# One graph-attention kernel: left and right projection as a 6x3x3-block product in 40 block products, in place of two 3x2x3 products in 15 each

## The chip, the cores and the metric

The kernel runs on one core of a Trainium2 chip. The metric is the device time of one execution in microseconds (us). Before the change it is 2752.59 us, the median of three runs (2751.57 to 2752.73).

## What is computed

128 graphs of 64 nodes with 768 features; two layers, then the input is added. All in float32. Of the reference only this matters here:

```python
h = max(layernorm(x), 0)
for l in range(2):
    m_left  = h @ W_left[l].T              # the two projections that are changed
    m_right = h @ W_right[l].T
    u_left  = h @ m_left^T / sqrt(768)     # 64 x 64 for each graph
    u_right = h @ m_right^T / sqrt(768)
    u = u_left on the upper triangle and the diagonal of adj, u_right below it
    attention = exp(u) * adj, rows scaled to sum 1
    h = relu(layernorm(attention @ (h @ W_lin[l].T + b_lin[l])) * ln_a[l] + ln_b[l])
out = x + h
```

## The kernel before

The engines are TensorE (PE; PEld is its weight loading), VectorE (DVE), ScalarE (ACT), GpSimd (POOL) and SyncE (SP, which issues the DMAs).

**Passes.** A layer has two passes over the 8192 tokens, in 16 blocks of 512. `pass_one` projects a block to the left and to the right, makes the scores (PE at L463, tile `aux`) and the softmax, and leaves the attention weights in DRAM. `pass_two` makes the linear projection (L852) and the product with the attention (`context`, L660, and `context_block`, L683), and normalizes. The second pass stays as it is, but for the places of its sums and loads.

**A projection as 15 block products.** Features are cut in three parts of 256, and a block of 512 tokens in two parts of 256, so a projection is a 3x3 matrix of weight blocks times a 3x2 matrix of token blocks: 18 block products. The kernel does it in 15, on sums and differences of blocks. `W_SUMS` makes 17 sums of weight blocks (L155, tiles `w_l`, `w_r`, `w_n`), `T_SUMS` 11 sums of token blocks (L155, tile `ts`, on POOL but in the first block), and `ORDER` lists the 15 products with the outputs that each one is added to or taken from. A product is four matmuls of 128x128 weights on 256 columns (L436). The right projection leaves out the last node of each graph, where the strict lower triangle has no use for it: 252 columns, in all blocks but the last. `read` (L203, L155) brings a PSUM sum into the tile `m`: the first contribution to an output is a copy on ACT, the others are additions on DVE (one operand in PSUM, one in SBUF).

**Order.** There is no automatic scheduler: instructions are issued as the Python code runs. `run(slot)` is called twice for each product and issues what `put` has entered for that slot, or the next entry of the list `idle`. So `prepare` sets the normalization of later blocks (`x`, statistics L238, transposes L380 into `xb`, the store `h<-xb` and the load `ht<-h`) beside the products. `one_aside` and `two_aside` put the loading and summing of later weights in `idle`, over many blocks. The scores of a block come after the first product of the next one. In layer 0 the first block's four token transposes on PE (L357) come ahead of its first product.

**End of a layer.** The scores of the last block follow its last product directly; then the linear products begin. The last context of layer 0 (L660) uses the PSUM places `aux`, which ACT and DVE read (L805, L823, L821) while the first products of layer 1 already run in `X`.

Of the kernel before, what the change touches and what calls it, by code (L numbers as in the profile page):

```python
# [17 lines left out]
def kernel(  # L18
# [12 lines left out]

# [37 lines left out]
    NBB = T // S  # L69
    adj_t = adj2.rearrange("(n h s) j k i -> n h j s (k i)", h=PAIR, s=Q)  # L70
# [9 lines left out]
    def put_all(slot, fs, step=1):  # L80
        for f in fs:
            if f is not None:
                put(slot, f)
            slot += step
        return slot

# [26 lines left out]
    FIRST = {0: ("X", 5), 1: ("Z", 8), 3: ("Y", 1), 5: ("V", 6), 9: ("V", 7), 12: ("V", 13)}  # L113
    W = {}
# [6 lines left out]
    def load_w(l, kind):  # L121
        v = SRC[kind][l].rearrange("(c p) o -> p c o", p=P)
        t = W[l, kind] = [wpool.tile([P, K2, D], F32, name=f"w_{kind}_{s}") for s in range(len(ORDER))]

        def load(s, i, j):
            nc.sync.dma_start(t[s], v[:, j * K2:(j + 1) * K2, i * D:(i + 1) * D])

        if (l, kind) in ((0, "l"), (0, "r")):
            return [lambda s=s, ij=ij: load(s, *ij) for s, ij in RAW.items()]
        return [lambda s=s, ij=ij: paced(t[s][:, 0, :1], lambda: load(s, *ij)) for s, ij in RAW.items()]  # L130

    def centre(l):

        t = W[l, "n"]
        for j in range(3):
            blocks = [s for s, (_, jj) in RAW.items() if jj == j]
            m = stat.tile([P, 3, K2], F32, name="wm", bufs=2)

            mean = stat.tile([P, K2], F32, name="wmm", bufs=2)
# [5 lines left out]
            idle.extend(none * (6 if j == 0 else 2))  # L145
            for n, s in enumerate(blocks):
                idle.append(lambda n=n, s=s, m=m: nc.vector.reduce_sum(m[:, n], t[s], axis=mybir.AxisListType.X))
            idle.append(mean_of)
            for s in blocks:
                idle.extend(none * 3)  # L150
                idle.append(lambda s=s, mean=mean: nc.gpsimd.tensor_sub(
                    t[s], t[s], mean.unsqueeze(2).to_broadcast([P, K2, D])))

# [3 lines left out]
    def sums_w(l, kind, eng):  # L157
        t = W[l, kind]
        return [lambda o=o, s=s, a=a, b=b: added(eng, t[o], s, t[a], t[b]) for o, s, a, b in W_SUMS]
# [9 lines left out]
    def tokens_of(key):  # L169
        ht = HT[key]  # L170
        r = {f"B{2 * j + t}": ht[:, j * K2:(j + 1) * K2, t * TH:(t + 1) * TH] for j in range(3) for t in range(2)}
        r.update(TS.get(key, {}))
        return r

    def sums_t(key, eng=nc.gpsimd):
        ts = TS[key] = {}

        def one(o, s, m, n):
            t = big.tile([P, K2, TH], F32, name="ts", bufs=13)
# [32 lines left out]
    KEPT = [[dram.tile([P, C, T], F32, name=f"h{l}_{u}") for u in range(NB)] for l in range(L)]  # L212
    ROWS = [dram.tile([NBB, S, H], F32, name=f"z_{u}") for u in range(NB)]
    ATT = [[dram.tile([P, Q, S], F32, name=f"att{l}_{u}") for u in range(NB)] for l in range(L)]
# [50 lines left out]

    def load_h(which, l, u):
        ht = HT[which, l, u] = big.tile([P, C, T], F32, name="ht")
        nc.sync.dma_start(ht, KEPT[l][u])

    def affine(which, l, u, step=1):  # L270

        def part(c0):
            for c in range(c0, c0 + step):
                ht = HT[which, l, u][:, c, :]
                nc.scalar.activation(ht, ht, AF.Relu, bias=cols[1][:, c:c + 1], scale=cols[0][:, c:c + 1])  # L275

        return [lambda c=c: part(c) for c in range(0, C if l else 0, step)]

    def transpose_rows(l, u, pool):

        key, xr, todo = (1, l, u), XR[l, u], []
        if l == 0:
# [24 lines left out]
            stats = [lambda q=q: mean_var(mv[:, q, :], [xr[q][:, :HH], xr[q][:, HH:]]) for q in range(Q)]  # L307
            norms = [lambda q=q: norm(q) for q in range(Q)]
            if u == 1:
# [3 lines left out]
                total, ss = (stat.tile([P, Q], F32, name=n, bufs=1) for n in ("total", "ss0"))  # L313
# [31 lines left out]
        if (l, u) == (0, 0):  # L345
            ht = HT[key] = big.tile([P, C, T], F32, name="ht")

            def turn(n, q):

                if n < 2:  # L350
                    p = ps_aux.tile([P, 2, T], F32, name="aux")
                    banks = [p[:, 0], p[:, 1]]
                else:
                    banks = [ps_st.tile([P, 2 * TH], F32, name=m) for m in ("XY", "ZV")[n - 2]]
                for m, p in enumerate(banks):
# [3 lines left out]
                for m, p in enumerate(banks):  # L359
                    to = ht[:, 3 * m:3 * m + 3].rearrange("p c (a g s) -> p g c a s", a=4, g=2)  # L360
                    to = to[:, q // 2, :, q % 2 * 2:q % 2 * 2 + 2, :]
                    (nc.vector.tensor_copy if n == 1 or n < m else nc.scalar.copy)(
                        to, p[:, :3 * P].rearrange("p (c a s) -> p c a s", c=3, a=2))

            for n, q in list(enumerate(START))[1:]:
                todo.append(lambda n=n, q=q: turn(n, q))
            todo.append(lambda: nc.sync.dma_start(KEPT[l][u], ht))
            return todo

        if (l, u) != (0, 1):  # L370
            xb = pool.tile([P, H // 32, Q, 32], F32, name="xb", bufs=1)

        def store():
            to = KEPT[l][u].rearrange("(b i) c t -> i c b t", b=4)
            for a in range(4):
                nc.sync.dma_start(to[:, :, :, a * P:(a + 1) * P],
                                  xb[a * 32:(a + 1) * 32].rearrange("i (c b) q j -> i c b (q j)", b=4))

        for q in range(Q):
            todo.append(lambda q=q: nc.vector.transpose(  # L380
                xb[:, :, q, :], xr[q].rearrange("p (b j) -> p b j", j=32)))
            todo.extend(none * ((l, u) != (0, 1)))
# [9 lines left out]
    def pass_one(l, aside):  # L392
        with tc.tile_pool(name=f"one{l}", bufs=2, reuse_waits="tile") as sp:
            ADJ, CHAIN, M = {}, {}, {}


            shapes = {"x": ([P, 2, H], 2), "xb": ([P, H // 32, Q, 32], 1), "m": ([P, C, NBB, 2, S], 1),
                      "adj": ([P, Q, 2, S], 2), "wm": ([P, Q, 2, S], 1)}
            places(sp, shapes, ("m", "adj", "x", "xb", "wm") if l else ("x", "xb", "m", "adj", "wm"))

            def load_adj(u):
                ADJ[u] = sp.tile([P, Q, 2, S], F32, name="adj")
                for h in range(PAIR):
                    nc.sync.dma_start(ADJ[u][h * S:(h + 1) * S].rearrange("p s k i -> p s (k i)"), adj_t[u, h])

            def softmax(u):
                return [lambda: next(CHAIN[u], None)] * 8

            def prepare(u):

                todo = transpose_rows(l, u, sp)
                todo.append(lambda: load_h(1, l, u))
                if u + 1 < NB:
                    todo.append(lambda: load_rows(l, u + 1, sp))
                todo.extend(softmax(u - 2) if u > 1 else [])
                todo.append(lambda: load_adj(u))
                todo.extend(none * ((9 if u > 1 else 15) if l else 0))
                return todo + affine(1, l, u)

            def project(u, k, just):  # L420


                b, w = lambda: tokens_of((1, l, u)), W[l, "lr"[k]]
                bank, seen = {}, set()


                ns = S - 1 if k and u < NB - 1 else S
                bs = "p (b s) -> p b s"
                for i, (at, t, _) in ((i, (o[1], o[2], o[3])) for i, o in enumerate(ORDER)):
                    new = i in FIRST  # L430
                    if new:
                        bank[at] = ps_st.tile([P, 2 * TH], F32, name=at)
                    p = bank[at][:, :NBB * ns].rearrange("p (g b s) -> p g b s", g=2, s=ns)
                    for g in range(2):
                        for c in range(K2):
                            nc.tensor.matmul(p[:, g], w[ORDER[i][0]][:, c, g * P:(g + 1) * P],  # L436
                                             b()[t][:, c, :].rearrange(bs, s=S)[:, :, :ns],
                                             start=(new and g == c == 0), stop=(c == K2 - 1), skip_group_check=True)
                        if g == 0:
                            run(30 * k + 2 * i)  # L440
                    if i == 0 and k == 0:
                        if u:
                            scores(u - 1)
                        M[u] = sp.tile([P, C, NBB, 2, S], F32, name="m", bufs=1)
                    read(p, lambda o: M[u][:, o // 2 * K2:(o // 2 + 1) * K2, o % 2 * 4:o % 2 * 4 + 4, k, :ns],
                         i, seen)
                    for f in just.get(i, ()):
                        f()
                    run(30 * k + 2 * i + 1)

            def scores(u):

                ht, m, adj = HT[1, l, u], M[u], ADJ[u]
                p = ps_aux.tile([P, 2, T], F32, name="aux")[:, 0].rearrange("p (q m) -> p q m", q=Q)
                for q in range(Q):
# [504 lines left out]
```

## Time and profile before

| | |
|---|---|
| median of 3 runs | 2752.59 us |
| profiled execution: span from first to last instruction | 2750.9 us |
| PE busy | 2730.4 us, 99% |
| DVE busy | 1345.6 us, 49% |
| POOL busy | 1194.4 us, 43% |
| ACT busy | 849.9 us, 31% |
| mean granted TensorE clock | 0.999 |

The profile gives for each engine the busy time and its groups of instructions (line, engine, operation, tile written <- tiles read, shapes, count; then the busy time, the mean of one in ns, and the idle time ahead of them with what ended it). The chain of waits goes from the last instruction back to whatever released each one. The timeline lists instructions in order of time: start, duration, engine, line, count, and in brackets the idle time before. An `x8` of PE in the chain is four matmuls with their four weight loads.

### The profile page before, as it was taken

The numbers are of one execution on the slowest core, as the hardware profiler recorded it, in microseconds if no ns is written. First come the engines' busy times: TensorE is split into PE (matmuls) and PEld (weight loads), VectorE is DVE, ScalarE is ACT, GpSimd is POOL, SyncE is SP. The second block draws the span as 40 slices with busy tenths as digits, with TensorE's granted clock in tenths as the row PEclk, the third lists the DMA queues.
The fourth block names the chain that finished last, engine by engine and source line by source line (L and its number), as shares of the span: only waits on it lengthen the run. The fifth ranks groups of instructions, "written<-read, shape, count | busy, mean of one in ns | idle before, by whom it ended". The sixth has DMA issues, their size and how long they took to land.

```text
span 2750.9 us, 46440 instructions
## 1 busy us (share of the span) xinstructions
PE 2730.4 (99%) x18746; PEld 2343.1 (85%) x18746; DVE 1345.6 (49%) x2266; ACT 849.9 (31%) x1612; POOL 1194.4 (43%) x937
## 2 busy tenths in 40 slices
PE   9999999999999999999999999999999999999998
PEld 8888888888888888888788888888888888888886
DVE  6555445545454333333435444444444335666667
ACT  3222223222221154444621211121122214544443
POOL 3332452223223555555522444223222325887886
PEclk9999999999999999999999999999999999999999
DMA  7434433343332333343555433443344205555555
GB/s 206 118 75 98 123 80 81 91 120 89 76 79 74 102 106 119 119 146 127 150 128 148 100 76 76 109 118 79 76 97 120 61 26 146 161 169 167 169 165 150
DMA packets 234072, 310.82 MB, mean 113 GB/s; under 512 B 54146, under 2 KB 184450, under 8 KB 225666
## 3 DMA queue, kind: packets, MB, share of 16 engines
q1 hardware_dynamic: 233698, 307.45, 41.8%
q8 instruction: 149, 2.44, 0.4%
q14 instruction: 65, 0.53, 0.1%
q10 hardware_dynamic: 160, 0.39, 0.0%
HBM read 202.91 MB, written 104.86 MB: 112 GB/s over the span
## 4 chain that ended last, share of the span: by engine, by line
PE 97%; DVE 1%; ACT 1%; DMA 0%; issue 0%; SPq 0%; DVEq 0%; ACTq 0%
PE X L436 24%; PE V L436 16%; PE X L852 12%; PE Y L436 12%; PE Z L436 8%; PE V L852 8%; PE Y L852 6%; PE aux L463 5%; PE Z L852 4%; PE aux L660 2%; PE aux L683 1%; PE Y L683 0%; ACT xb L316 0%; DVE wm L477 0%; DMA w_l<-in_w_left_dram 0%
## 5 line engine op out<-in xcount | busy, mean ns | idle before, releaser
L155 POOL TENSOR_TENSOR ts<-ht 128x512 f32<-128x512 f32 x441 | 587.0, 1341 | 1223.6 <-DMA ht<-h 565.1
L203 ACT ACTIVATE m<-X 128x512 f32<-128x512 f32 (+1 forms) x256 | 151.6, 592 | 1087.6 <-PE X L436 569.7
L155 POOL TENSOR_TENSOR ts<-ht,ts 128x512 f32<-128x512 f32 x189 | 248.7, 1323 | 135.6 <-PE X L852 60.5
L155 DVE TENSOR_TENSOR m<-m,V 128x512 f32<-128x512 f32 (+1 forms) x256 | 173.3, 677 | 269.1 <-PE V L436 269.0
L155 DVE TENSOR_TENSOR m<-m,X 128x512 f32<-128x512 f32 (+1 forms) x256 | 162.9, 677 | 248.0 <-PE X L436 247.4
L852 PE MATMUL X<-w_n,ts 128*128 128x256 f32 x1024 | 244.3, 380 | 0.8 <-ACT hl L203 0.6
L436 PE MATMUL X<-ts,w_l 128*128 128x256 f32 x1024 | 242.7, 380 | 0.1
L436 PE MATMUL X<-ts,w_r 128*128 128x252 f32 (+1 forms) x1024 | 238.8, 376 | 0.0
L155 DVE TENSOR_TENSOR m<-m,Z 128x512 f32<-128x512 f32 (+1 forms) x128 | 87.5, 683 | 307.7 <-ACT m L203 248.9
L852 PEld LDWEIGHTS X<-w_n,ts 128*128 128x128 f32 x1024 | 191.5, 190 | 33.3 <-issue 3.6
L436 PEld LDWEIGHTS X<-ts,w_l 128*128 128x128 f32 x1024 | 192.0, 190 | 30.1 <-DVE m L155 2.7
L436 PEld LDWEIGHTS X<-ts,w_r 128*128 128x128 f32 x1024 | 192.0, 190 | 26.0
L275 ACT ACTIVATE ht<-ht,b_col,a_col 128x512 f32<-128x512 f32 x192 | 143.5, 804 | 148.8 <-DMA ht<-h 148.8
L852 PE MATMUL Y<-w_n,ts 128*128 128x256 f32 x768 | 182.5, 379 | 0.0
L436 PE MATMUL Y<-ts,w_l 128*128 128x256 f32 x768 | 181.5, 379 | 0.6 <-DVE w_l L155 0.6
L436 PE MATMUL Y<-ts,w_r 128*128 128x252 f32 (+1 forms) x768 | 179.1, 376 | 0.0
L436 PEld LDWEIGHTS Y<-ts,w_l 128*128 128x128 f32 x768 | 145.8, 190 | 20.8 <-DVE w_l L155 1.0
L852 PEld LDWEIGHTS Y<-w_n,ts 128*128 128x128 f32 x768 | 145.8, 190 | 20.4 <-issue 0.6
L436 PEld LDWEIGHTS Y<-ts,w_r 128*128 128x128 f32 x768 | 145.9, 190 | 17.4
L155 DVE TENSOR_TENSOR hl<-hl,V 128x512 f32<-128x512 f32 (+1 forms) x136 | 89.1, 655 | 129.6 <-PE V L852 112.0
L818 POOL TENSOR_TENSOR z<-z,b 128x768 f32<-128x768 f32 x62 | 112.6, 1828 | 76.2 <-DVE z L815 76.2
L203 ACT ACTIVATE hl<-X 128x512 f32<-128x512 f32 (+1 forms) x135 | 77.9, 577 | 219.4 <-PE X L852 216.5
(167 smaller groups left out, 4737.1 us busy)
## 6 DMA issues: line engine op xcount, KB each, us to landing
ht<-h SPq DMA_DIRECT2D x63, 1536.0 KB, 7.1
h<-xb SPq DMA_DIRECT2D x124, 384.0 KB, 6.0
z<-z SPq DMA_DIRECT2D x128, 192.0 KB, 3.1
x<-z SPq DMA_DIRECT2D x128, 192.0 KB, 8.4
x<-in_x_dram SPq DMA_DIRECT2D x120, 192.0 KB, 8.3
xr<-in_x_dram SPq DMA_DIRECT2D x120, 192.0 KB, 3.8
out_dram<-xr SPq DMA_DIRECT2D x120, 192.0 KB, 2.7
adj<-in_adj_dram SPq DMA_DIRECT2D x64, 128.0 KB, 2.7
```

What stands on the lines that cost most here:

```text
L155: (eng.tensor_add if sign == "+" else eng.tensor_sub)(o, a, b)
L203: nc.scalar.activation(to(o), p, AF.Copy, scale=1.0 if sign == "+" else -1.0)
L275: nc.scalar.activation(ht, ht, AF.Relu, bias=cols[1][:, c:c + 1], scale=cols[0][:, c:c + 1])
L436: nc.tensor.matmul(p[:, g], w[ORDER[i][0]][:, c, g * P:(g + 1) * P], b()[t][:, c, :].rearrange(bs, s=S)[:, :, :ns], start=(new and g == c ...
L463: nc.tensor.matmul(p[h * S + e:h * S + e + 32, q, e:e + 95], ht[:, c, b * S + e:b * S + e + 32], mb[:, e:e + 95], start=(c == 0), stop=(c ...
L660: nc.tensor.matmul(cx[k][i, m, :HH], at[j, q, :], hl[j, q, m * HH:(m + 1) * HH], start=True, stop=True)
L683: nc.tensor.matmul(parts[r, k][n][i], at[j, q, :], hl[j, q, cut], start=True, stop=True)
L818: nc.gpsimd.tensor_add(zs[k], zs[k], rows["b"])
L852: nc.tensor.matmul(p[:, n], b[t][:, c, r * P:(r + 1) * P], w[s][:, c, :], start=(i in FIRST and i not in PRELOAD and n == c == 0), stop=(c ...
```

## The change

Left and right are now computed together: six rows of weight blocks (three left, three right) by three, times a 3x3 matrix of token blocks. That needs a superblock of 768 tokens and 54 block products, which `PRODUCTS` does in 40. The 16 blocks become 32 parts of 256 tokens: `SUPER[0]` is parts 0 and 1, done plainly in 36 products on the raw weights, and ten superblocks of three parts follow. The pieces:

- `W_OPS`: 101 sums of weight blocks, many with a factor, made once a layer from the 18 raw blocks. Class `Weights` gives them out while the plain block's products are issued, to DVE and POOL by two counted clocks (`turn_of`); those with a factor (51) go to DVE as `scalar_tensor_tensor`.
- `T_OPS`: 38 sums of token blocks for each superblock, all on POOL, at most 11 alive (class `Tokens`).
- `READS`: 84 contributions of products to the 18 outputs, 18 of them copies on ACT. The accumulators stay in PSUM over a superblock: product i goes on in bank i mod 4, with six banks in turn. So product i + 4 waits for the reads of product i.
- `m` becomes three tiles, `m0`, `m1`, `m2`. The scores of a superblock come after product 3 of the next one, and reads of products 0 to 3 after the scores.
- `REG`: 51 shared places of 128x512 for raw weights, weight sums, token sums and linear weights, handed on through the list `free`.
- The linear weights and the bias are loaded, centred and summed in the last superblock (`final`); centring moves from POOL to DVE and half of the 17 sums too.
- Left and right have all 256 columns. Token tiles, loads and stores go by parts; `aux` holds two of the six banks and the scores.

The diff, cut to its core (`...` marks what is left out; the tables are shortened to their first entries):

```diff
+    PRODUCTS = (
+        (74, 9), (71, 12), (82, 13), (78, 16), (72, 17), (67, 19), (73, 21), (89, 23), (75, 15), (76, 25), (60, 8),
...
+    READS = (
+        ((10, -2), (11, -1)), ((6, -2), (8, 1), (11, -1)), ((5, -1),), ((14, 1), (15, -1), (16, -2), (17, -2)),
...
+    T_OPS = (
+        (9, 4, 7, "-"), (10, 1, 7, "+"), (11, 2, 8, "+"), (12, 10, 11, "+"), (13, 3, 6, "-"), (14, 4, 5, "+"),
...
+    W_OPS = (
+        (18, 0, 1, 2, -1), (19, 8, -2, 5, 1), (20, 10, -2, 4, 1), (21, 6, -2, 3, 1), (22, 13, 1, 14, 1),
...
+    CHAINS, BANKS = 4, 6
+    SUPER = [(0, 1)] + [tuple(range(p, p + 3)) for p in range(2, NP, 3)]
+    PLAIN = 36
+    SCORED = 3
+    REGS = 51
+    REG = [wpool.tile([P, K2, D], F32, name=f"g{i}") for i in range(REGS)]
+    free = deque(REG)
...
+        def emit(self, eng, op):
+            v, a, ca, b, cb = op
+            x, y = self.at[a], self.at[b]
+            t, dead = self.place(v, a, b)
...
+            if ca == 1:
+                added(eng, t, "+" if cb > 0 else "-", x, y)
+            else:
+                nc.vector.scalar_tensor_tensor(t, x, float(ca), y, op0=ALU.mult,
+                                               op1=ALU.add if cb > 0 else ALU.subtract)
...
-            def project(u, k, just):
-                ns = S - 1 if k and u < NB - 1 else S
-                for i, (at, t, _) in ((i, (o[1], o[2], o[3])) for i, o in enumerate(ORDER)):
-                    new = i in FIRST
-                    if new:
-                        bank[at] = ps_st.tile([P, 2 * TH], F32, name=at)
...
-                    if i == 0 and k == 0:
-                        if u:
-                            scores(u - 1)
...
+            def turn_of(slot):
+                now = slot * 0.86
+                clock["vector"] = max(clock["vector"], now - 1.0) + sum(getattr(f, "vector", 0.0) for f in plan.get(slot, ()))
+                run(slot)
+                if weights.left and slot >= start["weights"]:
+                    while clock["vector"] <= now and weights.some(nc.vector):
+                        clock["vector"] += 0.62
+                    if clock["pool"] <= now and slot < start["tokens"]:
+                        if weights.some(nc.gpsimd, 40):
+                            clock["pool"] = max(clock["pool"], now) + 1.35
+                if clock["pool"] <= now + 1.5 and tokens.step(slot):
+                    clock["pool"] = max(clock["pool"], now) + 1.35
...
+            order = [(0, 0), (1, 0), (0, 1), (1, 1)] + [(w, t) for w in range(2, 6) for t in range(2)]
+            for n, (w, t) in enumerate(order):
+                if n == 2 and mid:
+                    mid()
+                bank = bank_of(n)
+                for j in range(3):
+                    tok = HT[1, l, t][:, j * K2:(j + 1) * K2, :]
+                    product(bank, weights.at[3 * w + j], tok, j == 0, slot)
...
+            for k in range(1, len(SUPER)):
+                put_all(slot + 2 * SCORED + 4, softmax(k - 1), 3)
+                if k == last:
+                    final(slot, tokens)
...
+                for i, (f, t) in enumerate(PRODUCTS):
+                    w, tok = weights.need(f), tokens.need(k, t)
+                    product(bank_of(CHAINS * (k - 1) + i % CHAINS), w, tok, i < CHAINS, slot)
+                    tokens.used(k, t)
...
+                    if i == SCORED:
+                        scores(k - 1)
...
+                    if i >= SCORED:
+                        for n in waiting:
+                            reads(n)
+                        waiting = []
+                    turn_of(slot + 1)
+                    slot += 2
...
+        def final(slot, tokens):
+            put_all(slot + 6, load_n(l), 2)
+            put(slot + 12, lambda: load_h(2, l, 0))
...
+            put_all(slot + 24, affine(2, l, 0), 2)
+            put_all(slot + 30, centre(l) + sums_n(l))
+            put_sums_t((2, l, 0), slot + 56, 2, slot + 50)
...
-    pass_one(0, {1: one_aside(0)})
-    pass_two(0, {1: two_aside("l"), 2: two_aside("r")})
-    pass_one(1, {1: one_aside(1)})
+    pass_one(0, {"weights": 7, "tokens": 58, 1: 13, 2: 38}, final_of(0))
+    pass_two(0, {11: lambda: later(load_raw(1), 1)})
+    pass_one(1, {"weights": 0, "tokens": 50, 1: 8, 2: 24}, final_of(1))
```

In the changed program the projection is at L619, the scores at L641, sums and additions at L231, weight sums with a factor at L523, reads with a factor 2 at L806, first reads at L802. A slot is half a product; a superblock has 80.

More of the change, by code (lines that the diff above doesn't have):

```diff
@@ L580, in pass_one, with bank_of @@
-            for f in list(idle):
-                if f:
+            KEEP["scores"] = KEEP["aux", 1]
+            def bank_of(n):
+                n %= BANKS
+                return KEEP["aux", 0][:, n] if n < 2 else KEEP["XYZV"[n - 2]]
+            flat = M[2].rearrange("p c b k s -> p (c b k s)")
+            spare = [flat[:, n * K2 * D:(n + 1) * K2 * D].rearrange("p (c d) -> p c d", c=K2) for n in range(6)]
+            weights, tokens = Weights(l, spare), Tokens(l)
+            clock = {"pool": 0.0, "vector": 0.0}
@@ L582, in pass_one @@
+            for n in sorted(plan):
+                for f in plan.pop(n):
                     f()
-            idle.clear()
             AHEAD.append(fresh(l, 0, (0, 1)))
-            scores(NB - 1)
-            for f in softmax(NB - 1):
+            scores(last)
+            for f in softmax(last):
                 f()
@@ L595, in bias @@
     def bias(l):
[L598 to L600 removed]
+        ab = [free.popleft() for _ in range(2)]
+        W[l, "bias"] = ab
+        t = rows["bias", l] = [ab[n // 2][:, n % 2, :] for n in range(4)]
+        todo = [lambda i=i, to=to: row(f"b{i}", b_lin[l], i * D, (i + 1) * D, t[to]) for i, to in enumerate((1, 2, 0))]
         bm = stat.tile([P, 3], F32, name="bm", bufs=1)
```

470 lines of the change are left out of this document (298 added, 172 removed), and 37 rows, old and new, of tables (PRODUCTS, READS, T_OPS, W_OPS).

## The prediction

> **What bounds the kernel now.** I read the page first: busy time, chain, engines' groups.
>
> ```profile
> span 2750.9 us, 46440 instructions
> PE 2730.4 (99%) x18746; PEld 2343.1 (85%) x18746; DVE 1345.6 (49%) x2266; ACT 849.9 (31%) x1612; POOL 1194.4 (43%) x937
> PE 97%; DVE 1%; ACT 1%; DMA 0%; issue 0%; SPq 0%; DVEq 0%; ACTq 0%
> ```
>
> TensorE (PE) is 99% busy and is 97% of the chain that ended last, so time falls only with PE's own work, and only while the others keep up. The chain in order of time gives the price of a product (four matmuls and four weight loads, hence x8) and of a block:
>
> ```profile
> 1486.32 4.06 PE aux L463 x192
> 1490.38 1.92 PE Z L436 x8
> 1492.30 1.73 PE X L436 x8
> 1494.03 1.73 PE Y L436 x8
> ...
> 1513.06 1.73 PE V L436 x8
> 1514.78 1.70 PE X L436 x8
> ...
> 1538.58 1.70 PE V L436 x8
> 1540.28 1.73 PE X L436 x8
> 1542.01 4.06 PE aux L463 x192
> ```
>
> From 1492.30 to 1513.06 lie 12 products of 256 columns: 1.73 us each. From 1514.78 to 1538.58 lie 14 of 252: 1.70. The scores take 4.06, and the product at 1490.38, the first behind them, 0.19 more than the rest. A block of 512 tokens comes to 55.69 us. PE waited for almost nothing:
>
> ```profile
> PE X L436 <- DVE w_l L155: 1.5, 1, 1.5
> PE Y L436 <- DVE w_l L155: 0.6, 1, 0.6
> PE V L436 <- DVE m L155: 0.3, 1, 0.3
> ```
>
> **What is removed from PE.** The built program issues 3488 projection matmuls of 256 columns in place of 2040 of 256 and 1800 of 252; scores (3072), linear and context stay. In units of a product (four): (2040/4) x 1.727 + (1800/4) x 1.70 - (3488/4) x 1.727 = 880.8 + 765.0 - 1505.9 = 139.9 us. There are 22 scorings, not 32, each with the 0.19: 1.9 us. The 2.4 us of startup waits above go: the first block multiplies raw weights; its start is read from these rows:
>
> ```profile
> 11.77 4.97 DMA w_r<-in_w_right_dram
> 10.98 1.01 DVE L362 COPY ht<-aux 128x384 f32<-128x384 f32 x2
> 11.52 0.49 PE L357 MATMUL Y<-ident,x 128*128 128x128 f32 x3
> 12.89 1.94 PE L436 MATMUL X<-ts,w_l 128*128 128x256 f32 x8
> ```
>
> It needs only the first two of four token transposes, whose copies are far enough at 11.6; the other two (four such rows, 1.9 us) now stand between its products: 13.5 against 12.9, 0.6 back. Together 143.6 us. Were nothing late the kernel would take 2752.6 - 143.6 = 2609.
>
> **What is added, steady part.** Per superblock PE works 40 x 1.727 + 6.1 + 0.2 = 75.4 us. POOL makes 38 token sums:
>
> ```profile
> L155 POOL TENSOR_TENSOR ts<-ht 128x512 f32<-128x512 f32 x441 | 587.0, 1341 | 1223.6 <-DMA ht<-h 565.1 <-ACT ht L275 413.9 <-DMA x<-z 98.3
> L477 DVE TENSOR_TENSOR wm<-aux,wm 32x380 f32<-32x380 f32 x128 | 70.1, 548 | 8.7 <-PE aux L463 7.3
> 31.32 1.28 DVE L155 TENSOR_TENSOR m<-m,X 128x512 f32<-128x512 f32 x2 [0.70 <-PE X L436]
> L380 DVE STREAM_TRANSPOSE xb<-x 128x768 f32<-128x768 f32 x124 | 116.6, 958 | 1.8 <-DMA x<-z 1.8
> 68.48 1.02 DVE L238 BATCH_NORM_STATS2 st<-x 128x6 f32<-128x384 f32 x2 [0.15 <-DMA x<-in_x_dram]
> ```
>
> 38 x 1.34 = 51 of 75 us: hidden. The tightest one (T_OPS 36) gets its place when product 18 ends and is due at product 20, one product of 1.73 us later, against 1.34. ACT's 18 first reads are light, and SP issues 1320 DMAs in the whole program, not 1240, spread as before: neither is near its limit. VectorE (DVE) adds the other 66 of 84 reads; two reads in a row take 1.28, 0.60 apart. That is 40 to 45 us, softmax some 8 (its four masks are 1.5 times as wide as the 548 ns ones), and 1.5 blocks of transposes (4 x 0.96) and, in layer 0, statistics (4 x some 1.2): about 13. Sum 61 to 66 of 75 in layer 0: covered, but bunched. The last four products of a superblock leave 4, 6, 4 and 6 reads to DVE: 20 x 0.60 = 12.0 us counted from the end of product 36. The scores, issued after product 3 of the next superblock, come 7 x 1.727 = 12.1 us after that point and start with m0, whose reads end 1.8 earlier. So slack is about 1.9 us. In layer 0 every other superblock has four row statistics shortly before; I add 1 us at five boundaries and 1 for the rest: 6 (0 to 20).
>
> **The 101 weight sums.** They were spread over whole blocks; now 75 or 76 stand on DVE and 26 or 25 on POOL, within one plain block, and in DVE's order all lie ahead of the first read that superblock 1 needs. Product 5 of that superblock waits for this read, since its bank is product 1's, and all other reads queue behind it. No gain is possible here: PE waited for no such sum before, but in the 2.4 us counted above. Both engines read two SBUF operands there. What that costs is seen at 35 us:
>
> ```profile
> 35.06 20.00 POOL L155 TENSOR_TENSOR w_r<-w_r,w_r 128x512 f32<-128x512 f32 x15
> 16.80 2.01 DVE L155 TENSOR_TENSOR w_l<-w_l,w_l 128x512 f32<-128x512 f32 x3
> 36.80 0.79 DVE L322 TENSOR_TENSOR nb<-total,rs 128x4 f32<-128x4 f32 x1
> 38.10 1.37 DVE L155 TENSOR_TENSOR w_r<-w_r,w_r 128x512 f32<-128x512 f32 x1
> 39.39 0.68 DVE L155 TENSOR_TENSOR m<-m,V 128x512 f32<-128x512 f32 x1
> 39.99 1.16 DVE L155 TENSOR_TENSOR w_r<-w_r,w_r 128x512 f32<-128x512 f32 x1
> ```
>
> With POOL idle, DVE sums are 0.67 each (2.01 for three). With POOL in its run of 15, two take 1.37 and 1.16, and a 128x4 product 0.79; a read from PSUM at 39.39 keeps its 0.68. So a DVE sum waits for the POOL sum under way. [...]
>
> Layer 1 (0.63 being between the pitch 0.60 of independent sums and the 0.67 of those that wait for one another): DVE 76 x 0.63 = 48, POOL 25 x 1.3 = 32, some 12 token sums already under way 15, transposes partly beside POOL: about 95 us. PE needs 62.2 + 5 x 1.727 + 4.1 = 75 from the same start to product 5. Stall 20 (0 with no exclusion: 48 + 8 = 56; 30 at worst). Layer 0: the transposes of block 2 are behind 59 weight sums in DVE's order: start 15 us (the last raw weights land at 16.7, the first ones earlier), 59 x 0.63 + 8 + most of 26 x 1.3 gives about 85. From transposes to loaded tokens the trace shows:
>
> ```profile
> 43.14 2.67 DVE L380 STREAM_TRANSPOSE xb<-x 128x768 f32<-128x768 f32 x3
> 45.84 5.23 SPq L376 DMA_DIRECT2D h<-xb  x4
> 57.71 0.35 SPq L268 DMA_DIRECT2D ht<-h  x1
> 64.78 2.50 POOL L155 TENSOR_TENSOR ts<-ht 128x512 f32<-128x512 f32 x2 [9.72 <-DMA ht<-h]
> ```
>
> 19 us from 45.81 to 64.78 for 1.5 MB; the needed part is half of it: I take 13.5. Then two token sums, 2.6: product 1 at 101, where PE would be at 77 (first product 11.6 + 1.9 for the transposes between + 36 x 1.727 + 1.7). Stall 24 (5 if nothing excludes: four token sums are due before product 1; 31 at worst).
>
> **Entry of layer 1.** The plain block's first sums use the aux place that the last context still occupies:
>
> ```profile
> 1377.06 1.99 PE L436 MATMUL X<-ts,w_l 128*128 128x256 f32 x8
> 1379.12 0.90 ACT L823 ACTIVATE z<-aux,rs 128x768 f32<-128x768 f32 x1 [0.50 <-DVE rs L811]
> ```
>
> 1380.0 - 1377.1 = 3 us of wait.
>
> **The last superblock of a layer.** The linear weights' loading, centring and sums move here from the idle slots of many blocks. In slots 30 to 68 (33 us) DVE has 32 reads (20 us), nine reductions (0.67 each, 6), small ones and a transpose 2, and 17 two-operand ops (9 centring, 8 sums, 0.6 each: 10); POOL is busy, so these wait 0.5 each, by the rows at 38.10 and 39.99: 8. That is 46 in 33: 13 late. Behind them come the bias (4) and the last 23 reads (14) in six products, 10.4 us: 8 more. The scores follow directly here, with no four products between.
>
> ```profile
> L147 DVE TENSOR_REDUCE wm<-w_n 128x2 f32<-128x512 f32 x18 | 11.7, 671 | 0.0
> 2265.12 1.89 PE L436 MATMUL V<-ts,w_r 128*128 128x256 f32 x8
> 2266.94 4.13 PE L463 MATMUL aux<-m,ht 128*32 128x95 f32 x192
> ```
>
> Before, they followed in step (2265.12 to 2266.94). Now 13 + 8 less the 1.8 by which m0 is early and some reads before slot 30 that finish ahead: 18 each layer (11 without exclusion, 25 if every op waits a whole POOL sum): 36.
>
> **Sum.** -143.6 + 24 + 20 + 3 + 36 + 6 = -54.6. The profiled span, 2750.9, lies 1.7 under the median of 2752.6; the terms are differences, so I take them from the median: 2698 us.
>
> **Rivals.** (1) The exclusion hardly matters: POOL's sums fall into DVE's gaps. Then layer 0 costs 5, layer 1 none, entry 3, ends 22, boundaries 6: 36, time 2645. For it: isolated DVE sums wait only half a POOL sum (1.16). Against: 75 in a row leave no gaps. (2) Slower: the scores wait at every one of 20 superblock boundaries because DVE carries a backlog into the last four products. Each microsecond there costs 20; it decides from 2.7 us a boundary (54.6/20), that is, from a backlog of 1.9 + 2.7 = 4.6 us at product 36. With 7 us: 20 x 5.1 - 6 on top, 2794. For it: DVE at 61 to 66 of 75 in layer 0, in bunches. Against: in slots 45 to 72 each product brings about 1.5 reads, 0.9 us of 1.73, so backlogs drain, and layer 1 has no statistics. (3) Products not removed: excluded, the instruction order shows 3488.
>
> **Chances.** Forecast 0.62, its own range 2665 to 2735; rival 1 0.23; rival 2 0.12; 0.03 for ending within 0.2% (5.5 us, about what a measurement of this kernel can tell from no change). The range 2635 to 2742 takes in rival 1 and stalls up to layer 0 31, layer 1 30, ends 50, boundaries 20 (entry 3 with them: 134 of the 143.6, 10 us under before), and leaves out rival 2. Faster 0.85, same 0.03, slower 0.12.
>
> **What would show it.** Right: PE busy some 140 us less; PE waits at the first superblock's products 1 to 5 for DVE or POOL in each layer (some 20 us), before the first linear product another 15 to 20, superblocks 75 us apart; DVE weight sums of 1.2 to 1.9 us beside POOL. Wrong: superblocks 78 us or more apart (rival 2), or weight sums at 0.67 and no waits (rival 1).

## The result, and the profile after

The changed kernel takes 3134.0 us (median of 4 runs, 3132.1 to 3136.1) against 2752.1 us before in the same runs: ratio 1.139 [1.137, 1.141]. It is 382 us slower, where 55 us less were forecast. The first view of the profile after is its page, with busy times, shares of the chain and the granted TensorE clock in forty slices:

```profile
span 3133.0 us, 46413 instructions
PE 2726.3 (87%) x18042; PEld 2277.2 (73%) x18042; DVE 1829.1 (58%) x2837; ACT 880.5 (28%) x1803; POOL 1700.9 (54%) x1301
...
PEclk8899999999999899999999989899899998999999
...
PE 45%; DVE 8%; SPq 4%; DMA 4%; ACT 2%; issue 2%; POOL 0%; DVEq 0%; ACTq 0%; POOLq 0%
```

PE is 45% of the chain that ended last, not 97%. It stands still for 3133.0 - 2726.3 = 407 us; before it was 20. And although by the prediction's count it has about 140 us less to do, it is busy as long as before (2730.4). In the clock row seven slices have fallen to 8 (0.8 to 0.9 of full speed), all of them in the two first passes; before, the row was 9 throughout. The mean granted clock over the span is 0.952, where it was 0.999. The row of the kernel before:

```profile
PEclk9999999999999999999999999999999999999999
```

So two things have to be found: what PE waits for, and why it runs slower. The waits view of PE (what waited, releaser, total us, times, longest) answers the first:

```profile
PE aux L619 <- DVE m L231: 207.4, 87, 6.4
PE aux L619 <- DVE m L806: 64.0, 32, 11.7
PE aux L619 <- POOL g L231: 37.1, 16, 12.7
PE Y L619 <- DVE m L231: 23.1, 3, 12.1
PE aux L619 <- ACT m L784: 22.3, 4, 16.2
...
PE aux L641 <- issue: 6.6, 8, 3.0
PE aux L641 <- DVE m L231: 6.0, 2, 3.5
...
PE X L619 <- DVE m L231: 1.2, 3, 0.6
PE V L619 <- DVE m L806: 0.8, 1, 0.8
```

Six places take the sums in turn, but nearly all waits of products (L619) are at `aux`, which is two of them: the two halves of one PSUM tile. X waits 1.2 us behind DVE in all. The scores themselves (L641) wait 12.6 us in all. The timeline (start, duration, instruction, and in brackets the wait and its releaser) shows one case, in layer 0:

```profile
715.28 1.89 PE L619 MATMUL aux<-g,g 128*128 128x256 f32 x8
...
715.96 1.32 DVE L669 TENSOR_TENSOR adj<-adj,s 128x384 f32<-128x384 f32 x1
717.20 0.68 DVE L806 SCALAR_TENSOR_TENSOR m<-X,m 128x512 f32<-128x512 f32 x1
...
720.68 1.25 DVE L806 SCALAR_TENSOR_TENSOR m<-aux,m 128x512 f32<-128x512 f32 x2
721.85 0.67 DVE L231 TENSOR_TENSOR m<-m,aux 128x512 f32<-128x512 f32 x1
722.58 3.78 PE L619 MATMUL aux<-ht,g 128*128 128x256 f32 x8 [5.41 <-DVE m L231]
```

The product at 715.28 goes into one half. DVE is late by some products, with the softmax and other sums ahead, and reads that half at 720.68 and 721.85. The next product goes into the other half, on which nobody works, and starts only when that last read is done. It then takes 3.78 us instead of 1.89: half rate. By the rotation superblocks 3, 6 and 9 of each layer use only X, Y, Z and V. In layer 0 they hardly suffer; the first matmuls of the scores of superblocks 2 to 5 show it:

```profile
323.48 6.47 PE L641 MATMUL aux<-m,ht 128*32 128x95 f32 x288
399.70 6.31 PE L641 MATMUL aux<-m,ht 128*32 128x95 f32 x288
498.76 6.26 PE L641 MATMUL aux<-m,ht 128*32 128x95 f32 x284
604.47 6.55 PE L641 MATMUL aux<-m,ht 128*32 128x95 f32 x288
```

76.2 us for superblock 3, where 75.4 were forecast; 99.1 and 105.7 for the next two. Superblocks 6 and 9 of layer 0 take 77.6 and 76.3. In layer 1 the three take 85, 90 and 81.5, still less than the others (98 to 113), so there something else adds to it.

### The profile page after: what moved, and what is told of

It is laid out like the page before. It is cut to its first block, busy times and chain, and to the rows that moved or that the text cites. A ratio compares the mean times of both kernels' runs of the same rounds, so it can differ in the third digit from the quotient of the medians.

```text
span 3133.0 us, 46413 instructions
## 1 busy us (share of the span) xinstructions
PE 2726.3 (87%) x18042; PEld 2277.2 (73%) x18042; DVE 1829.1 (58%) x2837; ACT 880.5 (28%) x1803; POOL 1700.9 (54%) x1301
## 4 chain that ended last, share of the span: by engine, by line
PE 45%; DVE 8%; SPq 4%; DMA 4%; ACT 2%; issue 2%; POOL 0%; DVEq 0%; ACTq 0%; POOLq 0%
PE X L1102 10%; PE V L1102 7%; PE aux L619 6%; PE Y L1102 5%; PE Z L1102 4%; DVE m L231 3%; PE X L619 3%; PE Y L619 2%; PE Z L619 2%; DMA ht<-h 2%; PE aux L641 2%; PE V L619 2%; PE aux L910 2%; DMA x<-z 2%; SPq L347 2%
## 5 line engine op out<-in xcount | busy, mean ns | idle before, releaser
L231 POOL TENSOR_TENSOR g<-ht 128x512 f32<-128x512 f32 x584 | 765.3, 1321 | 752.9 <-DMA ht<-h 342.8
L619 PE MATMUL aux<-g,g 128*128 128x256 f32 x1888 | 490.4, 407 | 233.2 <-DVE m L231 127.7
L619 PEld LDWEIGHTS aux<-g,g 128*128 128x128 f32 x1888 | 372.6, 202 | 324.4 <-POOL g L231 111.1
L231 POOL TENSOR_TENSOR g<-g,g 128x512 f32<-128x512 f32 x278 | 362.7, 1309 | 255.0 <-PE aux L619 115.5
L231 POOL TENSOR_TENSOR g<-ht,g 128x512 f32<-128x512 f32 x256 | 338.0, 1326 | 247.1 <-PE aux L619 97.7
L231 DVE TENSOR_TENSOR m<-m,aux 128x512 f32<-128x512 f32 x326 | 214.1, 683 | 338.2 <-PE aux L619 236.1
L619 PE MATMUL X<-g,g 128*128 128x256 f32 x1008 | 254.9, 398 | 1.2 <-DVE m L231 1.2
L619 PE MATMUL aux<-ht,g 128*128 128x256 f32 x544 | 160.3, 452 | 106.9 <-DVE m L231 79.7
L1102 PE MATMUL X<-g,g 128*128 128x256 f32 x1024 | 244.3, 380 | 4.9 <-ACT hl L286 2.5
L619 PEld LDWEIGHTS X<-g,g 128*128 128x128 f32 x1008 | 205.6, 205 | 36.2 <-POOL g L231 2.3
L619 PE MATMUL Y<-g,g 128*128 128x256 f32 x912 | 217.0, 381 | 8.8 <-POOL g L231 8.8
L619 PEld LDWEIGHTS aux<-ht,g 128*128 128x128 f32 x544 | 119.6, 226 | 141.2 <-DVE m L231 92.1
L1102 PEld LDWEIGHTS X<-g,g 128*128 128x128 f32 x1024 | 191.5, 190 | 37.4 <-issue 5.1
L802 ACT ACTIVATE m<-aux 128x512 f32<-128x512 f32 x128 | 70.3, 600 | 522.0 <-PE aux L619 248.7
L619 PE MATMUL Z<-g,g 128*128 128x256 f32 x864 | 208.4, 385 | 0.0
L619 PEld LDWEIGHTS Y<-g,g 128*128 128x128 f32 x912 | 174.3, 191 | 33.1 <-POOL g L231 9.2
L231 DVE TENSOR_TENSOR m<-m,Y 128x512 f32<-128x512 f32 x184 | 120.7, 680 | 113.2 <-ACT m L802 93.9
L619 PEld LDWEIGHTS Z<-g,g 128*128 128x128 f32 x864 | 167.5, 195 | 25.0
L1102 PE MATMUL Y<-g,g 128*128 128x256 f32 x768 | 182.5, 379 | 0.0
L619 PE MATMUL V<-g,g 128*128 128x256 f32 x768 | 181.6, 379 | 0.8 <-DVE m L806 0.8
L231 DVE TENSOR_TENSOR hl<-hl,V 128x512 f32<-128x512 f32 (+1 forms) x136 | 89.2, 656 | 130.0 <-PE V L1102 119.3
```

The source lines that it names most:

```text
L231: (eng.tensor_add if sign == "+" else eng.tensor_sub)(o, a, b)
L619: nc.tensor.matmul(p[:, g], w[:, c, g * P:(g + 1) * P], t[:, c, :], start=(new and g == c == 0), stop=(c == K2 - 1), skip_group_check=True)
L802: nc.scalar.activation(into(o), bank, AF.Copy, scale=float(c))
L1102: nc.tensor.matmul(p[:, n], b[t][:, c, r * P:(r + 1) * P], w[s][:, c, :], start=(i in FIRST and i not in PRELOAD and n == c == 0), stop=(c ...
```

## Experiments

Theory: a product into one half of the shared tile waits until the sum in the other half is read, and the clock falls behind such waits. Rivals: the tokens come late through SyncE's queue; VectorE has a backlog at the superblock boundaries (rival 2 of the prediction); VectorE and GpSimd hold each other up in the weight sums.

### Own places, loads first, both, and the weight sums on one engine

Own places (five tiles in turn; the plain block gets two separate aux tiles):

```diff
-    CHAINS, BANKS = 4, 6
+    CHAINS, BANKS = 4, 5
-                return KEEP["aux", 0][:, n] if n < 2 else KEEP["XYZV"[n - 2]]
+                return KEEP["aux", 0][:, 0] if n < 1 else KEEP["XYZV"[n - 1]]
```

> Edit: the superblocks rotate through five places, of which each is a PSUM tile of its own (one of aux, X, Y, Z, V), instead of six of which two are halves of one tile; the plain block likewise uses two separate aux tiles. Theory (shared place): a product into one half of aux waits until the sum in the other half has been read, which made 207 + 64 + 37 us of TensorE waits on aux in the changed kernel, and the granted clock falls behind such waits, which cost some 136 us more. Then the aux waits behind VectorE nearly vanish (under 60 us in all), and the time falls by 200 us or more, to 2750 to 2930. Rival A (late token loads): the weighted tokens come late from the DMA queue and the products wait for them under whatever name; then the aux waits go over to other places and the time stays above 3050. Rival B (VectorE's backlog at the boundaries): five places are scarcer than six, so the time stays or rises, 3100 to 3250.

2857.9 us, ratio 1.038 [1.035, 1.041]: 276 us gone. The engines' line of this kernel's page, then its waits of PE (waiter, releaser, total us, times, longest):

```profile
PE 2632.0 (92%) x18042; PEld 2231.9 (78%) x18042; DVE 1820.9 (64%) x2837; ACT 878.5 (31%) x1803; POOL 1704.1 (60%) x1301
```

```profile
PE V L619 <- DVE m L231: 27.6, 10, 12.3
PE X L619 <- DVE m L231: 26.9, 10, 11.8
PE X L619 <- POOL g L231: 22.1, 2, 19.1
PE Z L619 <- DVE m L231: 20.6, 8, 12.5
PE aux L619 <- DVE m L231: 20.1, 3, 12.0
```

The waits of aux behind DVE's sums (L231) fall from 207 us to 20, and PE busy by 94 us with the same matmuls. Layer 0 is at 75 to 79.5 us a superblock (the last one 91.7), near the 75.4 forecast; layer 1 still at 79 to 93, with one wait of 7 to 12.5 us in each of most superblocks.

Loads first (places for sums as in the changed kernel):

```diff
-                    put(end, lambda: load_rows(l, b + 1, sp))
+                    put(end + 4, lambda: load_rows(l, b + 1, sp))
-                    at = end + 3 + t
+                    at = end + 1 + t
```

> Edit: in the changed kernel, the load of the next tokens for GpSimd (h) is put on SyncE's queue ahead of the loads of rows (x and att) instead of behind them; places for sums as in the changed kernel. Theory (shared place): the waits on aux stay, so little changes: 3040 to 3130, with the wait of some 7 us at the superblocks that do not use aux gone. Rival A (late token loads): the waits of GpSimd for h (343 us in 34) and of ScalarE for it (270 us in 19) fall to under 100 us, and the time falls by 150 us or more, to under 2990.

3125.2 us, ratio 1.135 [1.133, 1.138]. Only 9 us gone: the order of the loads alone is not the cause. The waits behind the token loads moved little, GpSimd's from 343 us to 314 and ScalarE's from 270 to 217, where rival A expected under 100. Both edits:

> Edit: both, own places for sums and the token loads ahead of the row loads. Theory (shared place, with the loads as the second cause): superblocks come back to 75 to 80 us and the granted clock in the first passes to above 0.97; 2690 to 2780. If loads and places each hide the other, this falls clearly further than the sum of the two single edits. Rival B (VectorE's backlog at the boundaries, 2794 by the prediction): superblocks stay at 78 us or more with the first wait of each on VectorE; 2780 to 2850.

2843.6 us, ratio 1.032 [1.031, 1.034], 14 us under own places alone and above the 2690 to 2780 that the theory gave. Layer 1 now alternates between 75 to 78 and 87 to 89 us, but most of layer 0 went up to 80 to 86. Why, the timeline of this kernel shows, first in layer 0, then in layer 1:

```profile
334.25 0.33 SPq L352 DMA_DIRECT2D ht<-h  x1
334.69 6.88 SPq L347 DMA_DIRECT2D x<-in_x_dram  x8
...
344.57 1.02 DVE L322 BATCH_NORM_STATS2 st<-x 128x6 f32<-128x384 f32 x2 [6.38 <-DMA x<-in_x_dram]
...
346.31 0.68 DVE L231 TENSOR_TENSOR m<-m,Z 128x512 f32<-128x512 f32 x1
...
347.13 3.75 PE L619 MATMUL Z<-g,g 128*128 128x256 f32 x8 [3.36 <-DVE m L231]
```

```profile
1802.96 5.10 SPq L678 DMA_DIRECT2D att<-wm  x8
1808.10 5.20 SPq L467 DMA_DIRECT2D h<-xb  x4
1814.55 0.83 SPq L352 DMA_DIRECT2D ht<-h  x1
...
1824.55 3.06 ACT L363 ACTIVATE ht<-ht,b_col,a_col 128x256 f32<-128x256 f32 x6 [27.54 <-DMA ht<-h]
1827.51 0.57 ACT L806 ACTIVATE m<-Z 128x512 f32<-128x512 f32 x1
1828.12 0.69 DVE L231 TENSOR_TENSOR m<-m,Z 128x512 f32<-128x512 f32 x1 [11.37 <-ACT m L806]
1828.86 3.78 PE L619 MATMUL Z<-ht,g 128*128 128x256 f32 x8 [7.66 <-DVE m L231]
```

In layer 0 the row loads now stand behind the token load; DVE's statistics wait 6.4 us for them, the reads of sums queue behind the statistics, and PE waits 3.4 us for a place. In layer 1 the attention stores hold SyncE for 5.1 us ahead of the stores of h; ACT's affines wait 27.5 us for the tokens that follow, the first read of Z queues behind the affines, DVE waits 11.4 us for that read, PE 7.7 us for DVE. Each wait is handed on here because the waiting instruction stands in front. Whether it is this order, and not a backlog of VectorE, is tested below (order by layer).

Both edits and no weight sums on POOL (the lines for `nc.gpsimd` in `turn_of` left out, VectorE's clock 0.5 a sum, layer 0 from slot 2):

> Edit: as with both edits, and the sums of weights of both layers are made on VectorE alone, none on GpSimd, from an earlier slot in layer 0. Theory (VectorE and GpSimd slow each other in the weight sums: VectorE's sum of 128x384 took 1.08 to 1.2 us beside GpSimd's and 0.68 alone): VectorE's sums fall to about 0.7 us each and the first scores of each layer come as early as with both engines or up to 15 us earlier; time within 30 us of the run with both edits, on either side. Rival (no slowing; the sums are only divided): VectorE alone takes 1.4 times as long or more, each layer's first products stall by 20 us more, and the time is 30 to 60 us above the run with both edits.

2839.6 us, ratio 1.032 [1.030, 1.034], 4 us from the run with both edits. So two things fall. That the two engines hold each other up is not what made the kernel slow, since taking it away gains 4 us; and that they don't slow each other at all (the rival of this expectation) doesn't hold either, since some 25 more sums in each layer cost DVE no time (it is busy 1810.9 us in this run, 1817.3 in the run with both edits). (The sums are of 128x512, not of 128x384 as the expectation has it.)

### The halves of the shared tile apart

```diff
+            def bank_of(n):
+                n %= BANKS
+                return KEEP["aux", 0][:, n // 2] if n in (0, 2) else KEEP["XXXYZV"[n]]
```

(the plain block keeps the function that it had)

> Edit: the changed kernel with its six places and its shared tile, but the two halves of the tile are the first and the third place in the rotation, not the first and the second; the plain block and the queues' order are as in the changed kernel. So only one superblock in three uses both halves, with a product into X between them. Theory (a product waits until the sum of the other half, made just before, is read): waits on aux behind VectorE fall from 300 us to under 100, time 2840 to 2930, near the run with own places. Rival A (what mattered in that run was something else, such as the separate tiles of the plain block): the time stays above 3050.

2936.3 us, ratio 1.067 [1.065, 1.069]. Nothing but the order of the six places is changed, and 198 of the 276 us go. The aux waits behind DVE are 105 us, a little above the expectation, as is the time: where a superblock uses both halves, one product of some 1.7 us stands between them, and the waits on aux behind DVE's sums and reads go on, the longest 6.3 and 12.0 us:

```profile
PE aux L619 <- DVE m L231: 73.3, 43, 6.3
PE aux L619 <- DVE m L810: 32.1, 6, 12.0
```

### Filling the waits with needless work

```diff
+                    if i > 12 and (CHAINS * (k - 1) + i % CHAINS) % BANKS == 1:
+                        for _ in range(8):
+                            nc.tensor.matmul(KEEP["scores"][:, 1, TH:], KEEP["dummy"][:, :P], KEEP["dummy"], ...
```

> Edit: the changed kernel with its shared places, and eight needless matmuls of 128x256 ahead of each of some 98 products into the second half of the shared tile, in the places where TensorE waits. They add about 98 x 1.7 = 167 us of TensorE work and compute nothing that is used. Theory (the granted clock falls because TensorE stands still): the waits are filled, the granted clock in the first passes rises from 0.92 to 0.97 or more, and the time stays or falls, 3000 to 3134, in spite of the added work. Rival (the clock falls for another reason, such as the load): the clock stays, and the time is 3134 to 3300.

From the page, from the groups of instructions (busy time, mean ns of one), and from the waits:

```profile
span 3179.6 us, 49550 instructions
PE 2987.3 (94%) x19610; PEld 2538.3 (80%) x19610; DVE 1830.1 (58%) x2838; ACT 879.8 (28%) x1803; POOL 1702.5 (54%) x1301
```

```profile
L816 PE MATMUL aux<-dummy 128*128 128x256 f32 x1568 | 354.4, 379 | 0.0
```

```profile
PE aux L619 <- DVE m L231: 50.7, 38, 2.7
```

The number of places in the expectation was right, 98 with 784 matmuls, but their price was not. A projection matmul leaves two records of PE in these traces: the 3488 projection matmuls stand as 6976 records in the source view of L619, and the 784 as x1568. So an `x8` row is one product, four matmuls of two records each, and not four matmuls with their weight loads, as it was read ahead of the result. Eight needless matmuls cost two products, here 354.4 / 98 = 3.6 us, and not 1.7.

The time is 3181.0 us, 47 more: in the rival's range, above what the theory gave. But 354 us of work were added, not 167, and the clock rose, which the rival excludes. In the spans, PE stands still 214 us less (407 to 192), and the real work takes 2987.3 - 354.4 = 2633 us of busy time instead of 2726, 93 less; the mean clock is 0.978, not 0.952. 354 - 214 - 93 = 47. So here it is PE's standing still that lowers the clock, and not its load: with more load and shorter waits the clock is higher.

### Order by layer

Own places, the row loads ahead in layer 0 and the token loads ahead in layer 1; in layer 1 each third block is prepared 5 slots earlier, so that its stores of h stand ahead of the attention stores:

```diff
-                    put(end, lambda: load_rows(l, b + 1, sp))
+                    put(end + 4 if l else end, lambda: load_rows(l, b + 1, sp))
-                    at = end + 3 + t
+                    at = end + (1 if l else 3) + t
-                    (b, begins(1) + (18, 63, 103)[b % 3] + ...
+                    (b, begins(1) + (18, 63, 98 if l else 103)[b % 3] + ...
```

> Edit: five own places; the row loads go ahead of the token loads in layer 0 (as in the changed kernel) and behind them in layer 1; in layer 1 the third block of each three is prepared 5 slots earlier (98 instead of 103), so that its stores stand ahead of the attention stores on SyncE's queue, not behind them. Theory (what is left over after the shared place is head-of-line waiting on SyncE's queue: VectorE's row statistics behind row loads in layer 0, ScalarE's affines behind token loads in layer 1): superblocks of 76 to 79 us in both layers where the single orders gave 78 in one layer and 76/88 or 85/92 in the other; granted clock above 0.985; time 2735 to 2775. Rival (VectorE's backlog makes the long superblocks): the 88-us superblocks of layer 1 stay and the time is 2800 to 2850.

The page, and the first scores of three superblocks of layer 1 in the timeline:

```profile
span 2743.9 us, 46558 instructions
PE 2617.1 (95%) x18042; PEld 2223.2 (81%) x18042; DVE 1820.9 (66%) x2837; ACT 878.4 (32%) x1803; POOL 1703.5 (62%) x1301
```

```profile
1702.23 4.94 PE L641 MATMUL aux<-m,ht 128*32 128x95 f32 x232
1778.24 6.50 PE L641 MATMUL aux<-m,ht 128*32 128x95 f32 x288
1853.93 3.13 PE L641 MATMUL aux<-m,ht 128*32 128x95 f32 x140
```

2752.1 us, ratio 1.0003 [0.9994, 1.0013]: 91 us less than with both edits, and equal to the kernel before. The mean clock is 0.982, a little under the 0.985 expected. Superblocks are 75 to 78 us in both layers (here 76.0 and 75.7) but for the last. With the sums of weights on VectorE alone as well:

> Edit: as the run ordered by layer, and the sums of weights on VectorE alone. Theory: the two layers' first scores come some 3 and 17 us earlier, as they did with both edits (113 against 116 us; 557 against 577 us from layer 0's last scores to layer 1's first), so 2712 to 2750, faster than the kernel before. Rival (the gain of 17 us in layer 1 was lost again in its first superblock, 87 against 75 us, and is so here): within 8 us of the run ordered by layer.

2746.3 us, ratio 0.9985 [0.9975, 0.9994]: 6 us, within the rival's bound. The first scores of layer 1 come 18 us sooner, and 13 of these go again in its first superblock (87.9 against 74.9 us): DVE is still at the weight sums there, the first read of the superblock stands behind them, and the product at 1477.1 us waits 7.0 us for it.

### What is left at the ends

Layer 0's first sums waited for block 2 in the run with the sums on VectorE alone, by its timeline:

```profile
96.74 0.90 SPq L352 DMA_DIRECT2D ht<-h  x2
104.79 1.26 POOL L231 TENSOR_TENSOR g<-ht 128x512 f32<-128x512 f32 x1 [29.38 <-issue]
...
107.45 3.78 PE L619 MATMUL X<-g,g 128*128 128x256 f32 x8 [27.28 <-POOL g L231]
```

In layer 0, starting from that run, block 2's rows are now loaded ahead of block 1's stores, and its tokens ahead of block 3's rows:

```diff
+                ahead = (l, b) == (0, 1)
+                if ahead:
+                    todo.insert(-1, lambda: load_rows(l, b + 1, sp))
...
+                behind = l or b == 2
...
-                    put(end + 4 if l else end, lambda: load_rows(l, b + 1, sp))
+                    put(end + 4 if behind else end, lambda: load_rows(l, b + 1, sp))
...
-                    at = end + (1 if l else 3) + t
+                    at = end + (1 if behind else 3) + t
```

> Edit: as the run ordered by layer with the sums of weights on VectorE alone, and in layer 0 the rows of block 2 are loaded ahead of block 1's stores, and its tokens ahead of block 3's rows. Theory (what is left of layer 0's stall is the chain of block 2: rows, statistics, stores, tokens on SyncE's queue; the first sum of GpSimd waited to 104.8 us and TensorE 27 us for it): the tokens of block 2 land 8 to 13 us earlier, layer 0's first scores come at 102 to 108 us instead of 115, and the time falls by as much, 2733 to 2740. Rival (the sums of weights, made on VectorE alone, are as late): the first scores stay at 112 us or later and the time within 4 us.

2736.6 us, ratio 0.9947 [0.9933, 0.9962]: 10 us gone. POOL's first sum of block 2 starts 11.5 us sooner, and the first scores come at 104 us; the timeline has

```profile
93.28 1.26 POOL L231 TENSOR_TENSOR g<-ht 128x512 f32<-128x512 f32 x1 [23.15 <-issue]
```

And the bias rows in the last superblock off VectorE:

```diff
-                nc.vector.tensor_scalar_add(t[n], t[n], bs)
+                nc.scalar.activation(t[n], t[n], AF.Identity, bias=bs)
-            nc.vector.tensor_add(t[1], t[1], t[0])
+            nc.gpsimd.tensor_tensor(t[1], t[1], t[0], op=ALU.add)
```

(the second sum goes to GpSimd too, and the two negations to ScalarE)

> Edit: as the run with block 2 early, and the preparation of the bias rows in each layer's last superblock goes from VectorE to ScalarE (six operations of 128x256) and GpSimd (two). Theory (the last superblock is VectorE's backlog, 91.2 against 76.4 us and a wait of 9.6 us for the last sums): some 6 to 8 us leave VectorE there, the wait falls to 1 to 5 us in each layer, and the time falls by 8 to 16 us, to 2718 to 2732. Rival (another engine or the weights for pass two are last there): the wait stays, within 4 us of the run with block 2 early.

2729.1 us, ratio 0.9920 [0.9904, 0.9937], 7.5 us less than the run with block 2 early, slightly short of the 8 to 16; the last superblocks take 86.8 us instead of 91.2 to 91.5, and the longest wait before their scores is still 7.3. This version beats the kernel before by 22 us and the changed one by 405.

## Why the prediction was wrong

**The step that failed first** is in the steady part: "Per superblock PE works 40 x 1.727 + 6.1 + 0.2 = 75.4 us", "covered, but bunched", "So slack is about 1.9 us". Its term in the sum was 6 us, 20 at most. It counted for each product the reads of the same place four products earlier, as if each of the six places were waited for by itself. But two of them lie in one tile, and in the trace a wait for one half was a wait for all of it: the product at 722.58 us, into the second half, waited 5.41 us for the read of the sum that had ended just before in the first. So DVE's bunches, which four products of distance would have covered, stop PE at once. Taking the shared tile away was worth 276 us, and setting its halves apart in the rotation, with nothing else changed, 198. The 75.4 itself held: 76.2 in a superblock without the tile, 75 to 78 once places and queues were mended.

**The second step** is "ACT's 18 first reads are light, and SP issues 1320 DMAs in the whole program, not 1240, spread as before: neither is near its limit". Both are sums over the span. What counted was the order: a load that stands behind others on SyncE, an engine's first instruction waiting for it, and the reads of sums queued behind. With own places, both single orders left about 100 us in; the order by layer took 91 to 106 of them out. Under the shared tile the same reordering in one form showed as 9 us.

**The third** was left out entirely: the clock. The forecast took a wait of PE at its own length. Of the products in the timeline of the changed kernel (first passes of both layers), 26 of 27 behind a wait of over 3.5 us took more than 3 us instead of 1.9, 10 of 14 behind 2.5 to 3.5 us, and 6 of 104 behind shorter ones. PE busy is 2726.3 there and 2617.1 with the same matmuls in the run ordered by layer: 109 us. The trace's record of the granted clock fits the size (3.78 against 1.89): it has 53 stretches at half speed, and all but the last, at the end of the program, are 3.41 to 17.07 us long and begin during a wait of PE or within 2 us behind one. Nine of these 52 waits were shorter than 2.5 us, the shortest 1.9. So waits of two to three microseconds were paid too, if not each time.

**The other terms of the sum**, measured in the profiled run ordered by layer (the fastest of its ten), where the first two causes are gone: from the first product to the first scores layer 0 takes 104.4 us, of which 1.9 + 40 x 1.727 = 71.0 are work: stall 33 (24 forecast, 31 at worst). Layer 1: 96.3 - 69.1 = 27 (20, 30 at worst). Entry of layer 1: 3.8 (3). Eighteen superblocks lie 1.3 us above 75.4: 24 (6 forecast, 20 at most). The last superblocks, of 36 products and scores (68.5), take 91.2 and 91.3: 45 together (36; 22 to 50). That is 133.5, not 89, and -143.6 + 133.5 = -10 stands beside the -7.0 that the two spans show. The sum closes within 3 us, so the removed work fits as it was sized. The added stalls were put 44 us too low; the steady part and layer 0 lie beyond their own worst cases. Even without the two causes the change only draws level (2752.1 us).

**Rivals.** Rival 1 (the exclusion between DVE and POOL, a DVE sum waiting for the POOL sum under way, hardly matters) is out: DVE's largest group of weight sums in the first 115 us took 1078 ns each beside POOL's, 686 ns alone. These are the groups in the run ordered by layer and in the one with the sums on VectorE alone:

```profile
L523 DVE SCALAR_TENSOR_TENSOR g<-g,g 128x512 f32<-128x512 f32 x33 | 34.3, 1078 | 0.5
```

```profile
L523 DVE SCALAR_TENSOR_TENSOR g<-g,g 128x512 f32<-128x512 f32 x32 | 20.9, 686 | 0.4
```

So POOL's help was worth nothing here, which the prediction did not draw from it. That the two streams add up in full, as the stalls of 24 and 20 us have it, no run shows: in layer 0 of the run ordered by layer 75 sums of 0.60 us and 26 of POOL's of 1.3 would make 79 us, and DVE was busy 66 with its 75. Rival 2 (a DVE backlog at the boundaries) had the right sign and its mark came true ("78 us or more apart"), but not its mechanism: it let the scores wait, and they waited 12.6 us in the whole changed kernel. The products waited, at the shared tile, and in layer 0 that cost over 20 us in each superblock that used it, not 5 at its end. With own places and the order by layer a superblock lies 1.3 us above 75.4.

## What to carry to other kernels

Two accumulators in one tile were one accumulator to PE here (207 us of waits at aux behind DVE's sums, 20 with own places): check, for every place in a rotation, which tile its waits go by, and count the distance to the last read of the whole tile. Where a stream is 97% of one engine, price each new wait of that engine with the slow products behind it (here some 109 us of them beside 407 us of standing still), and look at the order on the DMA queue and in front of each engine's reads, not at how much they carry. A measured stall in one superblock with a regular pattern (here every third one fast) points to the cause more quickly than totals do.

## What was not expected of the hardware

A wait of PE cost more than its own length. Behind most waits of over some 3 us the next product took up to 3.78 us instead of 1.89, and in about half of these cases the one behind it 2.3 to 3.1. Over the span of the changed kernel PE was busy 109 us longer than with the same matmuls in the run ordered by layer, and some waits of only two microseconds, the shortest 1.9, were followed by half speed. 354 us of needless matmuls in the waits raised the mean clock from 0.952 to 0.978 and cost only 47 us of time.

And without GpSimd's help VectorE needed no more time for the weight sums. In layer 0 it was busy 66 us with its 75 sums of 128x512 beside GpSimd's 26 (run ordered by layer, lines 523 and 231), and 63 us with all 101 alone.
